# Two-layer graph kernel on one core: random-walk terms applied as R(x·U1 + R·x·U1'), and one stationary operand for q and k

## The chip, the cores and the metric

The kernel runs on one core of one Trainium2 chip. The metric is device time in microseconds; for the kernel before it is the median of three runs, 1678.13 us (1677.03 to 1678.82). One further execution was profiled, and every view of the trace comes from that one. Engines are named as the profile names them: PE is the matrix engine (TensorE), PEld its weight loads, DVE VectorE, ACT ScalarE, POOL GpSimd and SP SyncE, which here only issues transfers.

## The reference, cut to what matters

There are 2708 nodes with 256 features. The first layer mixes two kinds of propagation, a random walk R and a top-p attention A, over two steps; the second layer is a masked graph attention that the change does not touch.

```python
R = S + jnp.eye(N)
R = R / R.sum(-1, keepdims=True)
Z, Xf, Xa = 0, X, X
for n in range(2):
    q = Xa @ W1.T @ W2.T
    k = Xa @ W3.T
    A = top_p(softmax(q @ k.T), 0.9)     # rows cut to 90% of their mass, renormalised
    Xf = R @ Xf
    Xa = A @ Xa
    Z = Z + Xf @ U1[n].T + Xa @ U2[n].T
x = layernorm(X + layernorm(X + Z) * ln_g + ln_b)
# second layer: masked GAT attention over adj, then layernorm
```

So the walk's share of Z is R X U1[0] + R R X U1[1] (with U1 transposed), which is also R (X U1[0] + R (X U1[1])).

## The kernel before, in words

The 2708 rows are cut into 22 tiles, 16 of 128 rows and 6 of 110. Six groups of up to four tiles serve the transposes. The fast path of the first layer is `fast_layer0`; `general_layer0` is a fallback that does not run here.

**Prologue.** x is loaded to `xe`, whose 257th column is one. The loop at line 1039 takes each group: it transposes x (L1045), copies the result to SBUF on ACT and DVE, multiplies it by the stationary `wq` and then by `wk_sb` (L1056) and copies q and k out. `wq` and `wk_sb` each hold their 64 columns twice, so that q and k come out on both halves of the partitions: the scores split the keys in two halves, one on partitions 0 to 63 and one on 64 to 127, and q must stand beside both.

**Attention.** For each tile, `search` is a generator that is advanced one piece per slot: scores (L620) and their exponentials on ACT (L624), in step 1 also a survey on ACT and POOL and a bound on DVE, then candidates and a sort on DVE, and last one pass over the row (L794) that leaves the weights e and their sum. `weigh` then transposes e four tiles at a time (L202), copies the transposes on ACT (L208, `eT`) and multiplies by the features (L217, `att`). It turns group n+1 before it multiplies group n. After each of the six groups it calls `between`, and that calls `slot`. After the last one, ACT scales the result to `xa` (L1005) and the search of the tile three ahead begins.

**Walks.** The generator `walks` (L813) yields one 128-row block product at a time (L845): 2 steps x 22 tiles x 22 blocks = 968 units, each recorded as two matmuls. Its result is in `ps_wk`, a pool of one buffer. Blocks of the adjacency come by SP in half-tiles, one ahead, from a pool of three. In the first walk the moving operand is `xe` with its column of ones, so that the row sums come along; in the second it is `yw`.

**After the first walk** (`after_walk0`, L854): DVE adds the identity's part, `xf`, and takes the reciprocal of the row sum; PE transposes `xf` (L603, shared with the turning of `xa`), ACT copies it, PE multiplies it by both U1 side by side (`terms1`, L890), ACT scales both halves, and POOL adds the own part and x and stores the constant part to DRAM (`c1`). The second half is `yw`. The second walk begins when no such tile is unfinished.

**After the first attention** (`after_attention0`, L869): xa is turned; for every second tile `project` (L586, matmuls L591) makes q and k of the next step with the two stationaries; `terms2` (L905, L910) multiplies by both U2, leaving `ba`, the operand of the second attention, and `c2` in DRAM.

**After the second walk** (`finish`, L919): ACT scales the walk's result straight out of PSUM (L924), POOL sums it with `c1`, `c2` and the held attention result, and two layer norms follow, spread over slots by `yield`; `sources` then prepares the second layer.

**Order of the work.** It is written out by hand: `slot` advances the searches, may begin one, advances the tiles in `doing`, and then issues as many walk units as the slot is given; a walk's end closes the slot and the rest is owed to the next. The four compute engines execute in just this program order. The shares are:

- SPEND_FIRST: 5 units in each of the prologue's slots but the first.
- SPEND_0: 2, 2, 2, 2, 2, 1 for the six slots of a tile in attention step 0.
- SPEND_BETWEEN: 6 in the slots between the steps.
- SPEND_1: 5, 5, 4, 5, 5, 4 for a tile of step 1.

```python
while s and unfinished:
    yield True
...
owed[0] += spend
while owed[0] > 0:
    owed[0] -= 1
    if next(stream, True):
        break
```

Of the kernel before, what the change touches and what calls it, by code (L numbers as in the profile page):

```python
# [36 lines left out]
SPEND_FIRST, SPEND_0 = 5, (2, 2, 2, 2, 2, 1)  # L37
SPEND_BETWEEN, SPEND_1 = 6, (5, 5, 4, 5, 5, 4)
HELD = 8
# [6 lines left out]
def kernel(  # L46
# [71 lines left out]
    def load_x():  # L118
        step = 4
        for t0 in range(0, NT, step):  # L120
            by_tile(xe[:, t0:, 0:D], x, t0, min(t0 + step, NT))
# [103 lines left out]
    def general_layer0():  # L225
        with ExitStack() as l0:
# [8 lines left out]
            load_x()  # L235
# [248 lines left out]
    def fast_layer0(ep, adjp):  # L484
# [22 lines left out]
        wq = w0.tile([P, DC, 2, DA], F32, name="wq")  # L507
        wk_sb = w0.tile([P, DC, 2, DA], F32, name="wk_sb")
# [4 lines left out]
        w2_sb = tmp[:DA, P : 2 * P].rearrange("p (h e) -> p h e", h=2)  # L513
        w1_sb = heldp.tile([P, D], F32, name="xa1")[:DA].rearrange("p (c d) -> p c d", c=DC)
        nc.scalar.dma_start(w1_raw, w1T.rearrange("(c p) e -> p c e", p=P))
        for h in range(2):
            nc.scalar.dma_start(w2_sb[:, h, :], w2T)
        for h in range(2):
            nc.scalar.dma_start(wk_sb[:, :, h, :], w3T.rearrange("(c p) e -> p c e", p=P))
        load_x()  # L520
# [33 lines left out]
        yw = keep.tile([P, NT, D], F32, name="yw")  # L554
# [6 lines left out]
        c2 = [dram.tile([P, D], F32, name=f"c2_{t}") for t in range(NT)]  # L561

# [8 lines left out]
        for c in range(DC):  # L571
            tr = ps_tr.tile([P, 4, P], F32, name="tr")
            nc.tensor.matmul(
                tr[:, 0, :], w1_sb[:, c, :], w2_sb.rearrange("p h e -> p (h e)"),
                start=True, stop=True,
            )
            nc.vector.tensor_copy(wq[:, c].rearrange("p h e -> p (h e)"), tr[:, 0, :])

        def keep_k(s, c0, m, src, copy):
            low = max(0, min(HN - c0, m))  # L580
            if low:
                copy(kT[s][0:DA, c0 : c0 + low], src[0:DA, :low])
            if low < m:
                copy(kT[s][DA:P, c0 + low - HN : c0 + m - HN], src[DA:P, low:m])

        def project(s, c0, w, xT, copy_q, copy_k):  # L586

            pj = ps_tr.tile([P, 4, P], F32, name="tr").rearrange("p (n a) b -> p n (a b)", n=2)
            for n, wm in enumerate((wq, wk_sb)):
                for c in range(DC):  # L590
                    nc.tensor.matmul(  # L591
                        pj[:, n, :w], wm[:, c].rearrange("p h e -> p (h e)"), xT[:, c, :w],
                        start=(c == 0), stop=(c == DC - 1),
                    )
            copy_q(qT[:, c0 : c0 + w], pj[:, 0, :w])
            keep_k(s, c0, w, pj[:, 1], copy_k)
# [216 lines left out]
        def walks():  # L813
# [16 lines left out]
            for n, (s, t, j0, j1) in enumerate(queue):  # L830
                m = rows[t]
                cur, w = (xe, D + 1) if s == 0 else (yw, D)
# [5 lines left out]
                if j0 == 0:  # L838
                    ac = ps_wk.tile([P, CHUNK], F32, name="walk")
                    if s:  # L840
                        ca, cb = (finp.tile([P, D], F32, name=k) for k in ("ca", "cb"))
                        nc.sync.dma_start(ca[:m], c1[t][:m])
                        nc.sync.dma_start(cb[:m], c2[t][:m])
                for j in range(j0, j1):
# [4 lines left out]
                    if j == NT - 1:  # L849
                        doing.append(after_walk0(t, ac) if s == 0 else finish(t, ac, ca, cb))  # L850
# [3 lines left out]
        def after_walk0(t, ac):  # L854
            m = rows[t]
            unfinished.add(t)
            xf = rowp.tile([P, D + 1], F32, name="xf")
            nc.vector.tensor_add(xf[:m], ac[:m, : D + 1], xe[:m, t, :])
            nc.vector.reciprocal(rinv[:m, t : t + 1], xf[:m, D : D + 1])
            yield  # L860
            tp = ps_tr.tile([P, 4, P], F32, name="tr")
            xT = turn(xf, m, tp, nc.scalar.copy)
            yield
            terms1(t, xT)
# [4 lines left out]
        def after_attention0(t, xa):  # L869
# [10 lines left out]
            if t % 2:  # L880
                project(1, off[t - 1], 2 * m, both, nc.scalar.copy, nc.scalar.copy)
                yield
            terms2(t, xT)

        def terms1(t, xT):
# [3 lines left out]
            for c in range(DC):  # L889
                nc.tensor.matmul(  # L890
                    cy[:m], xT[:, c, :m], u_sb[:, 0, c].rearrange("p s e -> p (s e)"),
                    start=(c == 0), stop=(c == DC - 1),
                )
            r = rinv[:m, t : t + 1]
            cs = rowp.tile([P, D], F32, name="cs")
            nc.scalar.activation(cs[:m], cy[:m, 0:D], AF.Copy, scale=r)
            nc.scalar.activation(yw[:m, t, :], cy[:m, D : 2 * D], AF.Copy, scale=r)

            own = rowp.tile([P, D], F32, name="own", bufs=1)
            nc.gpsimd.tensor_scalar(own[:m], yw[:m, t, :], r, None, op0=ALU.mult)  # L900
            nc.gpsimd.tensor_add(cs[:m], cs[:m], own[:m])
            nc.gpsimd.tensor_add(cs[:m], cs[:m], xe[:m, t, 0:D])
# [16 lines left out]
        def finish(t, ac, ca, cb):  # L919
# [4 lines left out]
            nc.scalar.activation(xw, ac[:m, :D], AF.Copy, scale=rinv[:m, t : t + 1])  # L924
            yield
            while t not in held:
                yield
            hh = heldp.tile([P, D], F32, name="hh", bufs=4)[:m]
            nc.gpsimd.tensor_add(ca[:m], ca[:m], cb[:m])
            nc.gpsimd.tensor_add(ca[:m], ca[:m], held.pop(t)[:m])  # L930
            nc.gpsimd.tensor_add(hh, ca[:m], xw)
            yield
            for last in range(2):
# [4 lines left out]
                yield  # L938
# [3 lines left out]
                yield  # L942
# [6 lines left out]
                if not last:  # L949
                    nc.gpsimd.tensor_mul(hh, hh, g_sb[:m])  # L950
                    nc.gpsimd.tensor_add(hh, hh, b_sb[:m])
                    nc.gpsimd.tensor_add(hh, hh, xt)
# [6 lines left out]
        going, doing, unfinished = [], [], set()  # L959
# [33 lines left out]
        def step(s, cur, spend):  # L993
            for t in range(NT):
# [6 lines left out]
                def between(n):  # L1001
                    last = n == len(groups) - 1
                    if last:
                        xa = heldp.tile([P, D], F32, name="xa1")
                        nc.scalar.activation(xa[:m], ac[:m, :D], AF.Copy, scale=rden)  # L1005
                        if s:
# [31 lines left out]

# [273 lines left out]
```

## Time and profile before

| What | Value |
|---|---|
| median of three runs | 1678.13 us |
| the profiled execution: its time, its span | 1677.58 us, 1675.80 us |
| granted PE clock, mean | 0.992 |
| first transposition of attention step 0 starts | 70.46 us |
| last result xa of step 0 | 587.94 us |
| first transposition of step 1 starts | 653.75 us |
| last result xa of step 1 | 1280.04 us |
| one tile of step 0, one of step 1 | 22.3 or 26.1 us in turn; 28.5 us on average |
| walk units issued before step 0, in it, between, in step 1 | 44, 242, 97, 585 |
| POOL transfer c<-cs, issue to landing | 2.1 us |

Times are from the start of the span. The stages are told apart by the starts of the attention's instructions in the trace. A window gives, for each engine, its busy time and the number of its instructions in a stretch; a row of the timeline gives start, length, engine, line, operation and what it writes from what it reads, and in brackets the idle time before it with what ended that. The ends of matmuls are modelled, so a row of matmuls that overlap shows more busy time than they take; the distance from one start to the next does not have that flaw.

### The profile page before, as it was taken

The numbers are of one execution on the slowest core, as the hardware profiler recorded it, in microseconds if no ns is written. First come the engines' busy times: TensorE is split into PE (matmuls) and PEld (weight loads), VectorE is DVE, ScalarE is ACT, GpSimd is POOL, SyncE is SP. The second block draws the span as 40 slices with busy tenths as digits, with TensorE's granted clock in tenths as the row PEclk, the third lists the DMA queues.
The fourth block names the chain that finished last, engine by engine and source line by source line (L and its number), as shares of the span: only waits on it lengthen the run. The fifth ranks groups of instructions, "written<-read, shape, count | busy, mean of one in ns | idle before, by whom it ended". The sixth has DMA issues, their size and how long they took to land.

```text
span 1675.8 us, 23985 instructions
## 1 busy us (share of the span) xinstructions
PE 1610.0 (96%) x8218; PEld 1058.0 (63%) x8218; DVE 1217.0 (73%) x3660; ACT 766.8 (46%) x1324; POOL 423.4 (25%) x893
## 2 busy tenths in 40 slices
PE   7999999999999999999999999999997999999895
PEld 4677777777777776777787878777785222322332
DVE  2954554565455019888999999998994899888886
ACT  1333333333333255656576666667555334243231
POOL 0310111111011023223244444444434020420313
PEclk9999999999999999999999999999999999999998
DMA  6211011111110142212322322323222332232231
GB/s 166 73 47 46 26 43 40 40 31 40 40 43 25 43 104 67 63 49 73 79 72 79 87 68 82 89 58 77 72 65 88 98 99 86 88 93 77 76 86 39
DMA packets 153873, 113.89 MB, mean 68 GB/s; under 512 B 39898, under 2 KB 144094, under 8 KB 153742
## 3 DMA queue, kind: packets, MB, share of 16 engines
q1 hardware_dynamic: 149278, 105.18, 23.4%
q0 software_dynamic: 2112, 5.55, 1.0%
q10 hardware_dynamic: 2352, 1.54, 0.3%
q8 instruction: 67, 1.10, 0.3%
q14 instruction: 64, 0.52, 0.1%
HBM read 101.16 MB, written 11.09 MB: 67 GB/s over the span
## 4 chain that ended last, share of the span: by engine, by line
PE 78%; DVE 9%; ACT 5%; POOL 4%; issue 3%; DMA 0%; ACTq 0%; POOLq 0%; DVEq 0%; SPq 0%
PE att L217 23%; PE walk L845 19%; PE acc L1233 12%; PE acc L1240 6%; PE lg L620 5%; PE tr L202 4%; ACT e L624 3%; PE tr L910 2%; PE tr L890 2%; PE lg L1056 1%; PE tr L591 1%; DVE cand L725 1%; ACT eT L208 1%; DVE scr L791 1%; POOL res L1192 1%
## 5 line engine op out<-in xcount | busy, mean ns | idle before, releaser
L645 ACT ACTIVATE junk<-e,minus,rth 128x2708 bf16<-128x2708 f32 (+1 forms) x88 | 232.8, 2646 | 35.7 <-POOL rth L677 34.6
L845 PE MATMUL walk<-xe,blk 128*128 128x257 f32 (+3 forms) x968 | 240.5, 382 | 0.0
L217 PE MATMUL att<-ba,eT 128*128 128x256 f32 (+3 forms) x968 | 234.1, 383 | 5.0 <-ACT eT L208 5.0
L217 PE MATMUL att<-xe,eT 128*128 128x256 f32 (+3 forms) x968 | 233.3, 381 | 4.3 <-ACT eT L208 4.3
L208 ACT COPY eT<-tr 128x512 f32<-128x512 f32 (+5 forms) x264 | 138.2, 537 | 206.3 <-PE tr L202 206.1
L1233 PE MATMUL acc<-pt,v 128*64 128x512 f32 (+3 forms) x1056 | 226.0, 550 | 4.7 <-DVE pt L1225 3.8
L845 PE MATMUL walk<-yw,blk 128*128 128x256 f32 (+3 forms) x968 | 228.1, 381 | 1.7 <-ACT xw L924 1.7
L725 DVE MAX8 cand<-e 128x8 f32<-128x170 f32 (+1 forms) x352 | 89.2, 322 | 178.8 <-ACT e L624 178.8
L845 PEld LDWEIGHTS walk<-xe,blk 128*128 128x128 f32 (+3 forms) x968 | 174.6, 186 | 54.2 <-issue 29.3
L845 PEld LDWEIGHTS walk<-yw,blk 128*128 128x128 f32 (+3 forms) x968 | 176.7, 186 | 41.5 <-issue 11.5
L1225 DVE SCALAR_TENSOR_TENSOR pt<-e,tj,blk 128x1024 f32<-128x1024 f32 (+3 forms) x176 | 185.8, 1115 | 19.8 <-issue 8.0
L217 PEld LDWEIGHTS att<-ba,eT 128*128 128x128 f32 (+3 forms) x968 | 171.4, 186 | 32.7 <-ACT eT L208 10.0
L217 PEld LDWEIGHTS att<-xe,eT 128*128 128x128 f32 (+3 forms) x968 | 170.9, 186 | 30.9 <-ACT eT L208 7.2
L624 ACT ACTIVATE e<-lg 128x1024 f32<-128x1024 f32 (+1 forms) x132 | 121.1, 921 | 132.3 <-PE lg L620 132.3
L1233 PEld LDWEIGHTS acc<-pt,v 128*64 128x64 f32 (+1 forms) x1056 | 72.1, 137 | 153.5 <-issue 112.3
L202 PE MATMUL tr<-ident,e 128*128 128x128 f32 (+3 forms) x968 | 140.8, 270 | 4.6 <-ACT xT L606 3.8
L202 PEld LDWEIGHTS tr<-ident,e 128*128 128x128 f32 (+3 forms) x968 | 115.1, 139 | 32.3 <-ACT xT L606 6.1
L1165 ACT ACTIVATE blk<-blk 128x1024 f32<-128x1024 f32 (+3 forms) x66 | 63.2, 958 | 155.3 <-DMA blk<-in_adjT_dram 136.3
L1240 PE MATMUL acc<-pt,sb 128*32 128x512 f32 (+3 forms) x1056 | 124.5, 549 | 0.0
L1225 DVE SCALAR_TENSOR_TENSOR pt<-r,tj,blk 128x1024 f32<-128x1024 f32 (+1 forms) x88 | 109.8, 1306 | 10.8 <-issue 7.0
L631 POOL TENSOR_TENSOR fact<-zp 128x1 f32<-128x1 f32 (+1 forms) x44 | 24.8, 563 | 359.0 <-ACT e L624 349.1
L725 DVE MAX8 cand<-scr 128x8 f32<-128x97 f32 (+1 forms) x616 | 101.9, 243 | 0.0
(203 smaller groups left out, 1999.6 us busy)
## 6 DMA issues: line engine op xcount, KB each, us to landing
blk<-in_adjT_dram SPq DMA_DIRECT2D x32, 704.0 KB
blk<-in_adjT_dram SPq DMA_DIRECT2D x32, 512.0 KB
blk<-in_adjT_dram SPq DMA_DIRECT2D x48, 330.0 KB
blk<-in_adjT_dram SPq DMA_DIRECT2D x32, 320.0 KB
blk<-in_adjT_dram SPq DMA_DIRECT2D x12, 605.0 KB
blk<-in_adjT_dram SPq DMA_DIRECT2D x12, 440.0 KB
blk<-in_adjT_dram SPq DMA_DIRECT2D x18, 283.6 KB
c<-cs POOLq DMA_DIRECT2D x32, 128.0 KB, 2.1
```

What stands on the lines that cost most here:

```text
L202: nc.tensor.transpose(tr[: rows[t], q, :m], e[:m, off[t] : off[t + 1]], ident[:m, :m])
L208: copy(eT[:k, : len(grp), :m], tr[:k, : len(grp), :m])
L217: nc.tensor.matmul(acc, eT[: rows[t], q, :m], value(t), start=(t == 0), stop=(t == NT - 1),)
L620: nc.tensor.matmul(lg[:m, h, :w], qT[part, cols], kT[s][part, c0 : c0 + w], start=True, stop=True,)
L624: nc.scalar.activation(halves[:m, :, c0 : c0 + w], lg[:m, :, :w], AF.Exp, accum_out=zp[:m, n : n + 1],)
L645: nc.scalar.activation(junk[:m], e[:m], func, scale=rth, bias=minus1[:m], accum_out=acc)
L725: nc.vector.max(cand[:, n, :], src[:m, n * size : min(N, (n + 1) * size)])
L845: nc.tensor.matmul(ac[:m, :w], blk[: rows[j], j - j0, :m], cur[: rows[j], j, 0:w], start=(j == 0), stop=(j == NT - 1),)
L1165: nc.scalar.activation(bar, bar, AF.Sign)
L1225: nc.vector.scalar_tensor_tensor(pt[:k, :gw], r[h // 2][:k, h % 2, :gw], tj[:k, j, h : h + 1], mask, op0=ALU.max, op1=ALU.mult,)
L1233: nc.tensor.matmul(acc[h // 2][c][q * FO : (q + 1) * FO, :w], v[j][:k, h - 1 + q, :], pts[h - 1 + q][:k, c0 : c0 + w], **at,)
L1240: nc.tensor.matmul(acc[2][c][h * 32 : (h + 1) * 32, :w], sb[:k, j, h : h + 1].to_broadcast([k, 32]), pts[h][:k, c0 : c0 + w], **at,)
```

## The change

The walk is factored. In the prologue, x is loaded to a new tile `xm` instead of `xe`. The transposes of x stay in SBUF as `x_turned`, inside the still unused `ba`, and `terms1` runs for all 22 tiles in the prologue's ten slots, on x itself: its first half, x·U1[0], goes to `c1` in DRAM, and its second, x·U1[1], to `xe`. The first walk therefore carries x·U1[1]; its end, still a DVE add, is scaled by the reciprocal row sum on POOL and added to `c1` into `xm`. The second walk's operand is `xm`. The first attention reads x from `xm`, so the first walk may not end before it is done: no walk unit is issued in the prologue or in step 0, and the shares afterwards are larger.

`finish` now adds the identity's part out of PSUM on DVE and scales on ACT one slot later. It sums x (loaded anew), `c2` and the attention's result. Because the second walk trails the second attention, that result goes to DRAM (`c3`) for the first 18 tiles and is loaded back; the last four are held. Two `yield`s are gone from each of its two layer norms.

For q and k one tile `wkqk` holds W3, the product W1·W2, and W3 again. The stationary is the pair k|q for keys of the first half and q|k for those of the second, so one matmul group gives k on the partitions where it is needed and q on the others; a transfer issued by POOL then copies q to the partitions beside it.

```diff
-SPEND_FIRST, SPEND_0 = 5, (2, 2, 2, 2, 2, 1)
-SPEND_BETWEEN, SPEND_1 = 6, (5, 5, 4, 5, 5, 4)
-HELD = 8
+SPEND_BETWEEN, SPEND_1 = 7, (7, 6, 7, 7, 6, 7)
+HELD, WAITING = 6, 4
...
         nc.scalar.dma_start(w1_raw, w1T.rearrange("(c p) e -> p c e", p=P))
+        nc.scalar.dma_start(w2_sb, w2T)
         for h in range(2):
-            nc.scalar.dma_start(w2_sb[:, h, :], w2T)
-        for h in range(2):
-            nc.scalar.dma_start(wk_sb[:, :, h, :], w3T.rearrange("(c p) e -> p c e", p=P))
-        load_x()
+            nc.scalar.dma_start(wkqk[:, :, 2 * h, :], w3T.rearrange("(c p) e -> p c e", p=P))
+        xm = keep.tile([P, NT, D], F32, name="xm")
+        load_x(xm)
...
+        c3 = {t: dram.tile([P, D], F32, name=f"c3_{t}") for t in range(NT - WAITING)}
...
+        def project(s, c0, w, pj, xT, copy_q, copy_k):
+            for lo, hi, h in ((c0, min(c0 + w, HN), 0), (max(c0, HN), c0 + w, 1)):
+                if lo >= hi:
+                    continue
+                here, there = slice(h * DA, (h + 1) * DA), slice((1 - h) * DA, (2 - h) * DA)
+                at = slice(lo - c0, hi - c0)
                 for c in range(DC):
                     nc.tensor.matmul(
-                        pj[:, n, :w], wm[:, c].rearrange("p h e -> p (h e)"), xT[:, c, :w],
-                        start=(c == 0), stop=(c == DC - 1),
+                        pj[:, at], wkqk[:, c, h : h + 2].rearrange("p h e -> p (h e)"),
+                        xT[:, c, at], start=(c == 0), stop=(c == DC - 1),
                     )
-            copy_q(qT[:, c0 : c0 + w], pj[:, 0, :w])
-            keep_k(s, c0, w, pj[:, 1], copy_k)
+                copy_k(kT[s][here, lo - h * HN : hi - h * HN], pj[here, at])
+                copy_q(qT[there, lo:hi], pj[there, at])
+                nc.gpsimd.dma_start(qT[here, lo:hi], qT[there, lo:hi])
...
-                cur, w = (xe, D + 1) if s == 0 else (yw, D)
+                cur, w = (xe, D + 1) if s == 0 else (xm, D)
...
+                    ca = finp.tile([P, D], F32, name="ca", bufs=4)
                     if s:
-                        ca, cb = (finp.tile([P, D], F32, name=k) for k in ("ca", "cb"))
+                        cb = finp.tile([P, D], F32, name="cb")
+                        nc.sync.dma_start(ca[:m], x[off[t] : off[t + 1], :])
+                        nc.sync.dma_start(cb[:m], c2[t][:m])
+                        if t in c3:
+                            held[t] = finp.tile([P, D], F32, name="cc")
+                            nc.sync.dma_start(held[t][:m], c3[t][:m])
+                    else:
                         nc.sync.dma_start(ca[:m], c1[t][:m])
-                        nc.sync.dma_start(cb[:m], c2[t][:m])
...
             nc.vector.tensor_add(xf[:m], ac[:m, : D + 1], xe[:m, t, :])
-            nc.vector.reciprocal(rinv[:m, t : t + 1], xf[:m, D : D + 1])
+            nc.vector.reciprocal(r, xf[:m, D : D + 1])
             yield
-            tp = ps_tr.tile([P, 4, P], F32, name="tr")
-            xT = turn(xf, m, tp, nc.scalar.copy)
-            yield
-            terms1(t, xT)
+            nc.gpsimd.tensor_scalar(xf[:m, :D], xf[:m, :D], r, None, op0=ALU.mult)
+            nc.gpsimd.tensor_add(xm[:m, t, :], xf[:m, :D], ca[:m])
             unfinished.remove(t)
...
-            nc.scalar.activation(cs[:m], cy[:m, 0:D], AF.Copy, scale=r)
-            nc.scalar.activation(yw[:m, t, :], cy[:m, D : 2 * D], AF.Copy, scale=r)
-
-            own = rowp.tile([P, D], F32, name="own", bufs=1)
-            nc.gpsimd.tensor_scalar(own[:m], yw[:m, t, :], r, None, op0=ALU.mult)
-            nc.gpsimd.tensor_add(cs[:m], cs[:m], own[:m])
-            nc.gpsimd.tensor_add(cs[:m], cs[:m], xe[:m, t, 0:D])
+            nc.scalar.copy(cs[:m], cy[:m, 0:D])
+            nc.scalar.copy(xe[:m, t, 0:D], cy[:m, D : 2 * D])
             nc.gpsimd.dma_start(c1[t][:m], cs[:m])
...
-            nc.scalar.activation(xw, ac[:m, :D], AF.Copy, scale=rinv[:m, t : t + 1])
+            nc.vector.tensor_add(xw, ac[:m, :D], xm[:m, t, :])
             yield
+            nc.scalar.activation(xw, xw, AF.Copy, scale=rinv[:m, t : t + 1])
...
-                        if s:
+                        if s and t in c3:
+                            nc.gpsimd.dma_start(c3[t][:m], xa[:m])
+                            stored.add(t)
+                        elif s:
                             held[t] = xa
...
             for n in range(10):
-                slot(SPEND_FIRST if n else 0, (0, n // 4) if n in (0, 4, 9) else None)
+                slot(0, (0, n // 4) if n in (0, 4, 9) else None)
+                for t in range(n * NT // 10, (n + 1) * NT // 10):
+                    terms1(t, x_turned[:, :, off[t] : off[t + 1]])
             layer1_weights()
-            step(0, xe, SPEND_0)
+            step(0, xm, [0] * len(groups))
```

## The prediction, made before the result was known

> **What bounds the kernel now.** I read the head of the page first, then the busy rows by slice, then windows cut at the stage borders, and last the chain of waits in one stretch of each step. The head:
>
> ```profile
> PE 1610.0 (96%) x8218; PEld 1058.0 (63%) x8218; DVE 1217.0 (73%) x3660; ACT 766.8 (46%) x1324; POOL 423.4 (25%) x893
> ...
> PE   7999999999999999999999999999997999999895
> PEld 4677777777777776777787878777785222322332
> DVE  2954554565455019888999999998994899888886
> ```
>
> TensorE is near full throughout, and VectorE is half idle in attention step 0 (slices 3 to 13) and near full in step 1. The Trainium skill (Perfetto Trace Analysis, "Identifying the Most-Contended Engine") says that matmul busy time is a bad measure of headroom, and to use the weight-load share. By it TensorE has 37% free here, step 1 is VectorE's, and the change pays by spreading walks over VectorE-bound time: step 1 has 562.4 us of DVE work in 626.3. So I tested it with distances between starts, which no modelled end can spoil. Chain of waits, 880 to 900 us (start, length, what):
>
> ```profile
> 883.47 0.86 PE att L217 x4
> 884.34 1.92 PE lg L620 x8
> 886.26 0.37 PE tr L142 x2
> 886.63 1.73 PE walk L845 x8
> 888.36 0.45 PE tr L202 x4
> 888.83 0.59 ACT eT L208
> 889.47 1.99 PE att L217 x8
> ```
>
> A 256-wide fp32 matmul takes 1.73/8 = 0.216 us, a 128-wide transposition 0.11; a 512-wide one 0.43 (L910, 1.72 for four). Counts times these, by stage:
>
> ```profile
> core 0: us, PE busy (x) PEld busy (x) DVE busy (x) ACT busy (x) POOL busy (x), PEclk, DMA share, GB/s
> 0.00:70.46 70.46, 58.76 (x225) 36.18 (x225) 35.18 (x111) 16.73 (x32) 12.00 (x45) 1.00 0.50 130
> 70.46:587.94 517.48, 509.66 (x2443) 376.99 (x2442) 261.70 (x959) 171.94 (x386) 56.70 (x126) 1.00 0.14 39
> 587.94:653.75 65.81, 62.52 (x267) 43.80 (x266) 28.05 (x107) 36.06 (x51) 21.01 (x49) 1.00 0.38 98
> 653.75:1280.04 626.29, 615.24 (x3027) 482.70 (x3026) 562.37 (x2096) 402.25 (x659) 244.52 (x550) 1.00 0.27 70
> ```
>
> Step 0 (second row) holds 968 att (208.6 us), 484 walk (104.6), 484 tr (50.5), 232 score matmuls (43.7: pairs of 64 rows run side by side), 84 L910 (36.0), 44 L890 (18.9), 80 L591 (16.7) and 66 L603 (7.0): 486 of 517.5 us. The between stage comes to 59.4 of 65.8 and step 1 to 589 of 626.3. TensorE's own work fills 94% of layer 0; the row decides against the rule. A moved walk is then worth nothing by itself; a deleted matmul is worth its full length; and stalls (31.5, 6.5, 37 us) are what else can change.
>
> **What is deleted on TensorE.** (a) q and k from one stationary: in the prologue 24 of 48 L1056 matmuls, half of 18.1 us: -9.1. In step 0 and just after, 44 of 88 L591: -9.3. (b) xf is no longer turned: 44 L603 at 0.105: -4.6. (c) One weight transfer less ahead of the first copy; the ACT queue issues it in 0.6 us (two took 1.20): -0.6. The U1 product (88 L890) stays, in another place. Sum -23.6.
>
> **What moves, by stage.**
> Prologue: 70.5 - 0.6 - 9.1; out go 88 walks (-19.0), one L890 set (-1.7), two L603 (-0.2); in come 88 L890-like matmuls (22 tiles x 1.72 = +37.7); fewer seams, -1. It ends at 76.6. ACT has 0.75 us of copies per 1.72 us tile (two of 0.375, as L915/L916), so it hides. The two cs buffers come back after the copy, the issue and the landing (2.1 us for c<-cs): some 2.7 us, against 3.44 us for two tiles of TensorE; hidden, and if not, at most +5.
>
> Step 0: 517.5 - 104.6 (walks) - 18.9 (L890) - 2.3 (22 xf transpositions) - 8.3 (half of L591), and L890's seams, about -2. But the fillers go. The seam between two tiles, before:
>
> ```profile
> 306.37 1.99 PE L620 MATMUL lg<-junk,qT 64*128 64x512 f32 x8
> 307.54 1.03 ACT L624 ACTIVATE e<-lg 128x1024 f32<-128x1024 f32 x1 [0.59 <-PE lg L620]
> 308.56 1.02 ACT L624 ACTIVATE e<-lg 128x1024 f32<-128x1024 f32 x1
> 308.56 0.60 PE L845 MATMUL walk<-xe,blk 128*128 128x257 f32 x2
> 309.00 0.60 PE L202 MATMUL tr<-ident,e 128*128 128x128 f32 x4
> 309.81 0.61 ACT L208 COPY eT<-tr 128x512 f32<-128x512 f32 x1
> 310.47 1.99 PE L217 MATMUL att<-xe,eT 128*128 128x256 f32 x8
> ```
>
> ACT cannot make eT before both exponentials, so att waits until about 3.8 us after the first score matmul, whatever TensorE did meanwhile. Without the two walk matmuls (0.43) it idles 0.43 longer, over some 20 seams: +8.6. Inside a tile the copy (0.59, with 0.2 of latency) has 1.73 + 0.44 us of att and transpositions over it, so no filler is needed. Step 0 becomes 390.
>
> A rule speaks against this: TensorE: Matmul & The Clock Gate (Part 1) says that an idle window of about 3.4 us halves the clock. The PEclk column reads 1.00 with seams of some 0.6 us; the new ones are about 1 us, so I add nothing. By the rule, if gaps did reach it, attention's 16.5 us a tile would double where cold.
>
> Between: 112 half-columns of walk (3 + 13 slots of 7, 224 matmuls) for 97 (194): +6.5; four L890 sets -6.9, xf -0.9, L591 -0.8; the waits for xf vanish (-4.5), but the first search of step 1 took 52 us (601.9 to 653.75) and now has some 47 us of TensorE work over it (13 slots of 3.0 and 7 of scores), so +2 for the part that can't shrink (0 to +5). 61.2.
>
> Step 1: 1712 walks for 1170, +116.8; L890 -10.3, xf -0.9. Seams gain fillers (7, not 4 or 5, a slot): of the 8.1 us that att waits for eT I take 4 off, and 1.2 of L890's. The new wait: ps_wk has one buffer, and now VectorE empties it at all 44 walk ends. Behind that add queue the search steps on DVE, which wait with it; a late add holds the next walk, and in the second walk the scaling on ACT one slot later, with eT copies behind it. Bounds: 0 (adds in the first tiles of step 1 start 0.2 us after the walk, one 3.4) and 44 x 1.2 = 53 (an estimate: the slot with the sort holds six rounds of 0.75 us, L743 and L745, and some 2.5 of small operations, 7 us in all, against 3 us of walks and 2.2 of cover; half of such a lag over all slots). VectorE falls from 90% to about 77% of the step, so I take the nearer row: +2. 729.
>
> Hidden: the q copy by transfer. No row shows one within SBUF; nearest is c<-cs, 2.1 us, 0.65 of POOL. Its reader comes slots later (cover: over 10 us); if scores waited for the last, 0 to +3, and I take 0. POOL queues only tau and survey behind it and behind the c3 issue (waits for xa, 0.65 us for each of 18 tiles): hidden while a search has its two tiles of lead, else 18 x 0.65 = 12. SP's loads come two half-tiles ahead; the walks (44 x 1.39 MB over some 790 us) need 77 GB/s, and 104 went through in one slice. finish loses waits in issue order only; after 1280 us nothing changes: 395.8.
>
> Sum: 76.6 + 390 + 61.2 + 729 + 395.8 = 1652.6 of span, against 1675.8; with the 1.8 us around it (1677.58 - 1675.80) 1654.4. That run lies 0.6 below the median shown. I say 1654.
>
> **Rivals.**
> A, VectorE holds the walk's only PSUM buffer (slower). Place: the 44 walk ends, nearly all in step 1. Price 44 x 1.2 = 53 less the 2 taken: 1705. It outweighs the gain from 0.57 us a walk (25.2/44). For: DVE ran 93% busy from 800 to 1200 us. Against: "DVE e L794" held tr only 0.9 us in all, so VectorE does not trail TensorE by much.
> B, step 0 needs its fillers everywhere: each of 132 slots loses 0.15 us more, +20: 1674. For: the walks (104.6 us) were the only work in step 0 that waited for nothing there. Against: 2.17 us of cover for a copy of 0.8 in each slot.
> C, step 1 was held by VectorE more than starts show (stalls of 37 fall to 20): 1640. For: DVE's row of nines. Against: the 589 us count.
> D, the transfer of q delays each score, 44 x 2.1 less cover: under +3 as placed; inside the main case.
>
> **How the numbers follow.** Main 0.64 (own range 1645 to 1664), C 0.12, B 0.14, A 0.10. Unknown bounds (+5, +3, +12, seams +-9) widen the main case little. 1638 to 1675 leaves A's tail and little else out. A change of 0.2% (3.4 us) is about what measurement tells. Faster: main and C whole, B's half, A's small lags, 0.84; same 0.05; slower 0.11.
>
> **What would show it.** Right: L1056's group gone, one q/k matmul group of 44 in step 0; first tr near 77 us, step 0 ending near 467, step 1 beginning near 528 and ending near 1257; att idle before eT in step 0 doubled to 10 us or so; walk's idle on DVE xf/xw under 5. Wrong: a step-0 tile over 19 us (B), walk waiting on DVE over 20 us in all (A), clock under 0.95 in step 0, or scores released by a qT transfer.

## The result, and the profile after

The kernel after takes 1659.6 us (median of four runs, 1659.51 to 1660.77), the kernel before, on the same chip, 1678.08: a ratio of 0.9892 (95% interval 0.9875 to 0.9909), 18.5 us or 1.1% less. The forecast was 1654, with 1638 to 1675 as its range. The profiled run took 1660.77 us with a span of 1658.8, against 1652.6 in the sum. It is the slowest of the four, 1.2 us above their median, so about 1 us of the stage sums below may belong to this one execution.

The head of the page after and its busy rows:

```profile
PE 1585.9 (96%) x8114; PEld 1043.9 (63%) x8114; DVE 1227.9 (74%) x3682; ACT 754.0 (45%) x1304; POOL 424.0 (26%) x908
...
PE   7999999999999999999999999999998999999894
PEld 3476667666677887787778877887774232222332
DVE  3676667666408877867888888988874989889795
...
PEclk9999999999999999999999999999998999999997
```

TensorE is as full as before, with 104 fewer recorded matmuls. VectorE's row of nines in step 1 has become mostly sevens and eights: its work there is spread over a longer step. Windows cut at the stage borders of the kernel after (start and end, length, then busy time and count for each engine, the granted clock, DMA share and GB/s):

```profile
core 0: us, PE busy (x) PEld busy (x) DVE busy (x) ACT busy (x) POOL busy (x), PEclk, DMA share, GB/s
0.00:77.53 77.53, 66.47 (x199) 30.96 (x200) 39.18 (x123) 29.32 (x72) 18.84 (x67) 1.00 0.51 139
77.53:468.51 390.98, 372.60 (x1855) 269.83 (x1853) 249.78 (x920) 155.71 (x357) 31.85 (x95) 1.00 0.04 11
468.51:530.20 61.69, 59.33 (x263) 45.41 (x263) 28.56 (x110) 32.79 (x40) 15.71 (x43) 1.00 0.43 113
530.20:1255.62 725.42, 719.47 (x3534) 578.76 (x3533) 581.32 (x2140) 395.49 (x633) 274.71 (x582) 1.00 0.35 92
1255.62:1658.80 403.18, 368.08 (x2268) 118.92 (x2266) 329.08 (x390) 140.68 (x205) 82.91 (x121) 0.96 0.30 85
```

| stage | before, us | forecast | after | off by |
|---|---|---|---|---|
| prologue, to the first transposition of e | 70.5 | 76.6 | 77.5 | +0.9 |
| attention step 0 | 517.5 | 390 | 391.0 | +1.0 |
| between the steps | 65.8 | 61.2 | 61.7 | +0.5 |
| attention step 1 | 626.3 | 729 | 725.4 | -3.6 |
| after step 1 | 395.8 | 395.8 | 403.2 | +7.4 |

The first layer came out 1.2 us under its sum. The miss lies in the last row, of which the prediction said that nothing changes. VectorE's share of step 1 fell from 90% to 80% (581.3 of 725.4). Next come the groups that the prediction named. The first line is attention step 0 in the kernel before, the others are the kernel after (line, engine, operation, tiles, count, then busy time and mean ns, then idle time of the engine ahead of them and what ended it):

```profile
L217 PE MATMUL att<-xe,eT 128*128 128x256 f32 (+3 forms) x968 | 233.3, 381 | 4.3 <-ACT eT L208 4.3
...
L216 PE MATMUL att<-xm,eT 128*128 128x256 f32 (+3 forms) x968 | 229.3, 381 | 17.5 <-ACT eT L207 17.5
L216 PE MATMUL att<-ba,eT 128*128 128x256 f32 (+3 forms) x968 | 232.9, 381 | 5.4 <-ACT eT L207 5.4
L852 PE MATMUL walk<-xe,blk 128*128 128x257 f32 (+3 forms) x968 | 223.8, 382 | 1.9 <-DVE xf L866 1.8
L852 PE MATMUL walk<-xm,blk 128*128 128x256 f32 (+3 forms) x968 | 221.8, 380 | 0.0
```

The walks wait 1.9 us for VectorE in all, so the one buffer of `ps_wk` holds nobody up. The idle time ahead of `att` in step 0 is 17.5 us, where it was 4.3. A seam between two tiles of step 0 after, TensorE and ScalarE only:

```profile
274.99 1.99 PE L620 MATMUL lg<-junk,qT 64*128 64x512 f32 x8
276.22 1.03 ACT L624 ACTIVATE e<-lg 128x1024 f32<-128x1024 f32 x1 [0.65 <-PE lg L620]
276.90 1.09 PE L201 MATMUL tr<-ident,e 128*128 128x128 f32 x8
...
277.24 1.02 ACT L624 ACTIVATE e<-lg 128x1024 f32<-128x1024 f32 x1
...
278.23 1.07 ACT L207 COPY eT<-tr 128x512 f32<-128x512 f32 x2
278.87 1.99 PE L216 MATMUL att<-xm,eT 128*128 128x256 f32 x8 [0.88 <-ACT eT L207]
```

As forecast, `att` starts 3.9 us after the first score matmul. Both groups of transpositions are done by then and nothing else is left to issue.

### The profile page after: what moved, and what is told of

It is laid out like the page before. It is cut to its first block, busy times and chain, and to the rows that moved or that the text cites. A ratio compares the mean times of both kernels' runs of the same rounds, so it can differ in the third digit from the quotient of the medians.

```text
span 1658.8 us, 24037 instructions
## 1 busy us (share of the span) xinstructions
PE 1585.9 (96%) x8114; PEld 1043.9 (63%) x8114; DVE 1227.9 (74%) x3682; ACT 754.0 (45%) x1304; POOL 424.0 (26%) x908
## 5 line engine op out<-in xcount | busy, mean ns | idle before, releaser
L216 PE MATMUL att<-xm,eT 128*128 128x256 f32 (+3 forms) x968 | 229.3, 381 | 17.5 <-ACT eT L207 17.5
L1234 PE MATMUL acc<-pt,v 128*64 128x512 f32 (+3 forms) x1056 | 230.7, 555 | 5.1 <-DVE pt L1226 3.8
L852 PE MATMUL walk<-xe,blk 128*128 128x257 f32 (+3 forms) x968 | 223.8, 382 | 1.9 <-DVE xf L866 1.8
L852 PE MATMUL walk<-xm,blk 128*128 128x256 f32 (+3 forms) x968 | 221.8, 380 | 0.0
L216 PEld LDWEIGHTS att<-xm,eT 128*128 128x128 f32 (+3 forms) x968 | 171.2, 186 | 44.8 <-ACT eT L207 22.3
L852 PEld LDWEIGHTS walk<-xm,blk 128*128 128x128 f32 (+3 forms) x968 | 177.7, 186 | 32.7 <-issue 4.9
L201 PEld LDWEIGHTS tr<-ident,e 128*128 128x128 f32 (+3 forms) x968 | 113.7, 139 | 45.1 <-PE lg L620 14.5
L866 DVE TENSOR_TENSOR xf<-walk,xe 128x257 f32<-128x257 f32 (+1 forms) x22 | 9.4, 426 | 112.4 <-PE walk L852 112.4
```

The costliest lines, as they stand in the source:

```text
L201: nc.tensor.transpose(tr[: rows[t], q, :m], e[:m, off[t] : off[t + 1]], ident[:m, :m])
L216: nc.tensor.matmul(acc, eT[: rows[t], q, :m], value(t), start=(t == 0), stop=(t == NT - 1),)
L852: nc.tensor.matmul(ac[:m, :w], blk[: rows[j], j - j0, :m], cur[: rows[j], j, 0:w], start=(j == 0), stop=(j == NT - 1),)
L1234: nc.tensor.matmul(acc[h // 2][c][q * FO : (q + 1) * FO, :w], v[j][:k, h - 1 + q, :], pts[h - 1 + q][:k, c0 : c0 + w], **at,)
```

## The experiments

Eleven kernels were run, each against the kernel before on the same chip. "To acc" is from the end of step 1 to the second layer's first accumulating matmul (`acc`), "rest" from there to the end. The five stage columns are from the profiled run, in us. The kernel before took 1677.1 to 1678.1 us (medians) on the chips used, so a difference of 1 us between two rows says little without the trace.

| run | median | ratio to before (95%) | prologue | step 0 | step 1 | to acc | rest |
|---|---|---|---|---|---|---|---|
| before | 1678.08 | | 70.5 | 517.5 | 626.3 | 18.1 | 377.6 |
| after | 1659.60 | 0.9892 (0.9875-0.9909) | 77.5 | 391.0 | 725.4 | 15.6 | 387.5 |
| apart | 1673.25 | 0.9974 (0.9963-0.9985) | 86.1 | 398.3 | 725.4 | 15.0 | 383.7 |
| stationary | 1660.24 | 0.9898 (0.9882-0.9913) | 61.9 | 510.1 | 626.3 | 18.0 | 377.0 |
| seam | 1638.52 | 0.9764 (0.9751-0.9778) | 77.8 | 369.1 | 725.6 | 15.6 | 387.2 |
| targets | 1665.82 | 0.9932 (0.9918-0.9945) | 77.5 | 391.0 | 725.4 | 24.2 | 382.6 |
| queue | 1658.17 | 0.9881 (0.9866-0.9896) | 77.5 | 391.0 | 725.4 | 15.7 | 385.7 |
| twice | 1668.66 | 0.9940 (0.9927-0.9954) | 84.4 | 390.9 | 725.5 | 15.6 | 388.7 |
| spread | 1658.91 | 0.9889 (0.9874-0.9904) | 78.1 | 391.0 | 725.4 | 15.2 | 385.5 |
| all | 1635.08 | 0.9744 (0.9730-0.9757) | 77.8 | 369.1 | 725.4 | 15.7 | 384.3 |
| warm | 1657.50 | 0.9880 (0.9865-0.9895) | 77.8 | 391.0 | 725.5 | 14.5 | 384.9 |
| pinned | 1663.76 | 0.9916 (0.9903-0.9930) | 77.9 | 390.9 | 725.4 | 25.6 | 381.6 |
| all_warm | 1633.45 | 0.9738 (0.9724-0.9751) | 77.3 | 369.1 | 725.5 | 14.5 | 382.9 |

### Which half of the change carries the gain

**apart** takes the q and k half out of the kernel after:

```diff
-        wkqk = w0.tile([P, DC, 3, DA], F32, name="wkqk")
+        wq = w0.tile([P, DC, 2, DA], F32, name="wq")
+        wk_sb = w0.tile([P, DC, 2, DA], F32, name="wk_sb")
...
-                nc.gpsimd.dma_start(qT[here, lo:hi], qT[there, lo:hi])
```

> The kernel after, with the two stationaries for q and k back (512-wide products for q and for k, no transfer of q); walks stay factored. Theory 1 (deleted TensorE work is worth its full length, a moved walk nothing): +9.1 us before the first score and +9.3 us in step 0 and the stretch behind it, +0.6 us for one more weight transfer, so about 1678 us (1674 to 1682), the time of the kernel before. Theory 2 (the 18 us come from the walks' new place and from the ends of the walks, the q and k products were hidden beside other engines' work): 1660 to 1666 us. In both the stretch after step 1 stays near 403 us.

**stationary** puts only that half into the kernel before, the same lines the other way round.

> The kernel before, with q and k from one stationary and q copied by the transfer; walks as before, nothing moved. Theory 1: 1678.1 - 18.4 - 0.6 = about 1659 us (1656 to 1663), all of the change's gain, and the stretch after step 1 stays near 396 us as in the kernel before; so the walks' factoring comes out at nothing, its deleted transpositions being eaten by empty tile seams and a longer second layer. Theory 2: 1668 to 1677 us.

The second is what theory 1 said, to 1 us: 1660.24, no different from the whole change. Its stages are shorter by 8.5 us (prologue), 7.3 (step 0), 0.7 (between) and 0.7 (after step 1), and step 1 does not move. So one stationary for q and k by itself gives the time of the whole change, and the walks' factoring adds nothing to it. That nothing is two amounts that cancel. Against this run, the kernel after has 15.6 us more in the prologue, 119.2 less in step 0, 3.4 less between and 99.2 more in step 1, which is 7.8 less in the first layer; and it has 8.2 more after step 1. Together +0.4.

The first run fell between the theories: 1673.25 instead of 1678, so the factoring alone does gain, 3.9 us against the kernel before on the same chip. Without the one stationary the first layer loses 16.7 us (8.6, 7.3, 0.7), near theory 1's 19.0, but behind step 1 the run takes 4.5 us less than the kernel after. That pointed to the end of the program, taken up below.

### The seam of step 0

**seam** moves the second product of each tile (`terms2`, 1.7 us of TensorE) from inside the tile into the next tile's seam, between the first two groups of transpositions and the first `att`, with its result in the walk's PSUM buffer, which is free in step 0:

```diff
-            terms2(t, xT)
+            if t < NT - 2:
+                late.append((t, xT))
+            else:
+                terms2(t, xT)
...
                 ahead = turned(n + 1)
+            if seam and n == 0:
+                seam()
```

> The kernel after; in step 0 the second product of each tile (terms2: two 512-wide matmuls with their weights, about 1.7 us of TensorE) is issued between the first two groups of transpositions of the next tile and its first attention matmul, where TensorE waits about 1 us for ScalarE's eT; same work in all. Theory 1 (the seam is empty TensorE time, 20.9 us over 20 tiles beyond the matmuls' own lengths): the stall goes almost whole, 1639 to 1646 us, and step 0 ends about 18 us sooner. Rival (ScalarE or VectorE sets the pace of a step-0 tile, so the wait comes back elsewhere in the tile): 1656 to 1661 us.

The result is 1638.52, 21 us below the kernel after and half a microsecond under the range of theory 1, and step 0 is 21.9 us shorter with the same work in it. One seam of this run:

```profile
245.58 1.99 PE L622 MATMUL lg<-junk,qT 64*128 64x512 f32 x8
247.50 1.09 PE L201 MATMUL tr<-ident,e 128*128 128x128 f32 x8
248.43 1.88 PE L924 MATMUL walk<-u_sb,xT 128*128 128x512 f32 x4
248.85 1.07 ACT L207 COPY eT<-tr 128x512 f32<-128x512 f32 x2
250.14 1.89 PE L218 MATMUL att<-xm,eT 128*128 128x256 f32 x8
```

The product runs under ScalarE's exponentials and copies; `att` follows with no wait. Summed, the wait for eT is gone, and inside the tile, where the product used to lie, none has come in its place:

```profile
L218 PE MATMUL att<-xm,eT 128*128 128x256 f32 (+3 forms) x968 | 227.3, 379 | 0.8 <-ACT eT L207 0.8
```

So a step-0 tile is TensorE's, and needs work in the seam only. That is the term "+0.43, over some 20 seams" of the prediction together with the stall that was there before: counted as the prediction counts, step 0 had 31.5 us of stalls in the kernel before and has about 38.5 in the kernel after. Filling the seam is worth more than the whole change. How much the same filler would gain in the kernel before, no run says.

### After step 1: three causes for 7.4 us

From step 1's end, before against after: the first `acc` comes 2.5 us earlier (15.6 for 18.1); from it to the last of the 264 `pt` operations of VectorE that feed the matmuls it takes 358.1 us for 351.0 (+7.1); from there to the end 29.5 for 26.7 (+2.8). Together +7.4. The 7.1 come in two places: +3.0 by the 22nd `pt` and +4.5 between the 44th and the 66th; what follows gives 0.4 back. With the end of the program that is three places to explain.

**The clock behind the seam.** Windows around the first `acc` (1271.23) in the kernel after (columns as in the stage windows: TensorE's time and count come first, the granted clock is third from the end):

```profile
1263.00:1267.00 4.00, 0.53 (x4) 0.12 (x3) 3.23 (x6) 1.14 (x7) 1.73 (x2) 1.00 0.62 182
1267.00:1271.00 4.00, 2.57 (x6) 1.20 (x6) 4.00 (x4) 1.30 (x8) 0.00 (x0) 0.50 0.23 34
1271.00:1275.00 4.00, 3.77 (x10) 1.25 (x12) 2.96 (x3) 2.28 (x4) 0.00 (x0) 0.50 0.77 250
1275.00:1279.00 4.00, 4.00 (x20) 0.89 (x20) 0.00 (x0) 1.11 (x4) 0.00 (x0) 0.72 0.72 207
```

TensorE is empty for 3.5 us behind step 1, and then the granted clock is 0.50 for 10.2 us (1267.0 to 1277.2). Ten matmuls fit into the four microseconds of the third row. The kernel before had one such stretch between step 1 and its first `acc`, of 3.4 us, behind 3.9 us of empty TensorE:

```profile
1284.00:1288.00 4.00, 0.51 (x5) 0.27 (x3) 2.67 (x5) 1.14 (x7) 3.83 (x6) 1.00 0.73 216
1288.00:1292.00 4.00, 3.38 (x11) 2.42 (x12) 2.67 (x4) 2.13 (x10) 2.59 (x3) 0.57 0.21 68
```

This fits the rule of the Trainium skill (TensorE: Matmul & The Clock Gate, Part 1) that an idle window of about 3.4 us drops the array to half clock; the prediction held it only against step 0, where the rows above agree with it by showing 1.00 for gaps of 0.9 us. The figure is not a safe limit, though. In the second layer TensorE waits 2.5 us for VectorE at one place, in the kernel before as in the kernel after; behind it the clock fell for 3.4 us in the first and stayed at 1.00 in the second:

```profile
1582.00:1586.00 4.00, 4.00 (x8) 0.93 (x7) 2.47 (x7) 0.00 (x0) 2.70 (x4) 0.57 0.10 33
```

```profile
1563.00:1567.00 4.00, 4.00 (x15) 1.22 (x15) 2.48 (x6) 0.00 (x0) 2.59 (x4) 1.00 0.10 33
```

Of the thirteen traces, six show the half clock at that place.

**warm** adds work to test it: 24 transpositions into a buffer that nobody reads, where TensorE waits for the last tile.

```diff
+            if t == NT - 1:
+                busy = ps_tr.tile([P, 4, P], F32, name="tr")
+                for n in range(24):
+                    nc.tensor.transpose(busy[:, n % 4, :], ident, ident)
             yield from sources(t, rowp, ps_tr)
```

> The kernel after, and 24 transpositions of the identity into a buffer that nobody reads, put ahead of the last tile's sources, where TensorE waits 3.5 us behind step 1: work added, none removed, the order of the rest kept. Theory 5 (the 3.5 us of empty TensorE bring 10.2 us of half clock, of which 6 us lie over the second layer's first accumulating matmuls and cost about 3 us): no stretch of half clock between the end of step 1 and the first matmuls, from the first accumulating matmul to the end about 384.5 us instead of 387.5, time 1656 to 1657.5 us. Rival (the clock falls for another reason, or VectorE sets those first neighbours): 1659 to 1662 us.

It gave 1657.5, faster by 2.1 us with more to do. The intervals of the two ratios overlap, but each of its four runs (1657.07 to 1658.73) is below each of the four of the kernel after (1659.51 to 1660.77). The same windows of this run:

```profile
1263.00:1267.00 4.00, 3.42 (x28) 3.01 (x26) 3.23 (x5) 1.14 (x7) 1.73 (x2) 1.00 0.69 195
1267.00:1271.00 4.00, 2.05 (x10) 1.06 (x12) 4.00 (x5) 1.49 (x8) 0.00 (x0) 1.00 0.27 56
1271.00:1275.00 4.00, 4.00 (x28) 1.16 (x28) 3.31 (x3) 1.70 (x2) 0.00 (x0) 1.00 0.84 294
```

The clock stays at 1.00, 28 matmuls fit where there were ten, and the first 22 `pt` take 24.37 us from the first `acc`, as in the kernel before (24.37; 27.35 in the kernel after). The first `acc` comes 1.1 us earlier too, since the last tile's `sources` run at full clock. So the pause is shown to be the cause of the half clock here, and the half clock of the +3.0.

**The second span's targets.** 32 transpositions into `aux` and 16 exponentials on ScalarE were all in the seam behind step 1 before, in seven pieces between the work of the last tiles' `sources`. After, the scheduler, which orders what lies behind the hand-written part, put 8 in the seam and left 24 among the `acc` matmuls of the first span, where the code has them. The last eight before, and the 24 after:

```profile
1295.13 0.60 PE L174 MATMUL aux<-ident,s_src 128*128 128x128 f32 x4
1295.72 1.14 PE L148 MATMUL tr<-wx,xT 128*110 128x264 f32 x4
1296.70 0.60 PE L174 MATMUL aux<-ident,s_src 128*128 128x128 f32 x4
1298.14 1.08 PE L1233 MATMUL acc<-pt,v 128*64 128x512 f32 x4 [0.83 <-issue]
```

```profile
1334.02 1.09 PE L173 MATMUL aux<-ident,s_src 128*128 128x128 f32 x8
1335.04 1.07 PE L1234 MATMUL acc<-pt,v 110*64 110x512 f32 x2
1336.22 1.20 PE L173 MATMUL aux<-ident,s_src 128*128 128x128 f32 x8
1337.35 1.08 PE L1234 MATMUL acc<-pt,v 110*64 110x512 f32 x4
1338.36 1.09 PE L173 MATMUL aux<-ident,s_src 128*128 128x128 f32 x8
```

**targets** holds all of them ahead of the first `acc`, on TensorE and ScalarE, in an order held through the first two neighbours:

```diff
+        r_next = [rp.tile([P, 2, GW], F32, name=f"r{q}") for q in range(2)]
+        pinned = ExitStack()
+        pinned.enter_context(tc.manual_schedule(engines={nc.tensor.engine, nc.scalar.engine}))
+        list(targets(1, r_next, aux))
...
```

> The kernel after; the second layer's targets of its second span (32 transpositions and 16 ScalarE exponentials) are held ahead of the second layer's first accumulating matmul, as the kernel before had them, in the seam where TensorE waits for the second layer's first operands. Theory 1 (their late place, with VectorE waiting 4.9 us for ScalarE's masks, is the larger part of the 7.4 us that the stretch after step 1 is longer than predicted): 1654 to 1657 us, that stretch 398 to 400 us. Rival (the 7.4 us are TensorE's half clock after the seam, or a longer start): 1658 to 1662 us.

This was a miss: 1665.82. From the first `acc` on it is 4.9 us shorter, but the first `acc` comes 8.6 us later: the masks of the second layer stood behind the exponentials on ScalarE, and VectorE waited 13.75 us for one. **pinned** holds TensorE alone, for the first neighbour:

```diff
...
+        pinned.enter_context(tc.manual_schedule(engines={nc.tensor.engine}))
...
```

> The kernel after; on TensorE alone all 32 target transpositions of the second span are held ahead of the first accumulating matmul (8 and 24), ScalarE's order is left free, so that masks come between the exponentials. Theory 4: the 4 us that they cost inside the first span go, and the first accumulating matmul comes 2 to 4 us later since the last of them wait for ScalarE to empty their two buffers: net 0 to -2, 1657.5 to 1660 us. Rival (as in the run with both engines held, the seam pays for all of it): 1663 to 1666 us.

It was slower again, 1663.76, with the first `acc` 9.9 us later and 5.9 us saved behind it; in the seam TensorE waited 6.4 us for ScalarE to empty the buffers. So the seam was not free for them in one block. **spread** gives one tile of targets to each of eight neighbours:

```diff
+                if g == 0 and n == 3:
+                    r_next = [rp.tile([P, 2, GW], F32, name=f"r{q}") for q in range(2)]
+                    later = targets(1, r_next, aux)
+                if g == 0 and n >= 3:
+                    next(later, None)
...
```

> The kernel after; the second layer's targets of its second span (8 tiles, each four transpositions and two ScalarE exponentials) are spread over the fourth to the eleventh neighbour of the first span, one tile each, instead of 8 transpositions in the seam and 24 in one place. Theory 4: clustered, the 16 exponentials hold ScalarE's masks back and VectorE waits 4.9 us; spread, they lie beside 5.5 us of VectorE per neighbour, so from the first accumulating matmul to the end 383 to 385 us instead of 387.5 and the time 1655 to 1657 us. Rival (this stretch is TensorE's, and the transpositions cost the same anywhere): 1659 to 1661 us.

It gave 1658.91, 0.7 us below the kernel after, within the interval. In its trace two of the eight tiles still lie in the seam and six in the span, four transpositions each. The first half clock lasted 6.8 us, not 10.2 (-1.0 by the 22nd `pt`), and the stretch from there to the 66th took 63.5 us for 64.5, where the kernel before takes 60.0. The theory was mostly wrong: VectorE's 4.9 us of waiting was worth 1.0, and 3.5 stay wherever the transpositions lie inside the span. The rival was nearer, and starts show why: each of the six groups puts 1.10 us between two pairs of `acc` matmuls that otherwise start 0.42 apart, 6 x 0.68 = 4.1 us of TensorE. In the kernel before their place in the seam cost nothing behind the first `acc`, and its seam was only 2.5 us longer; no run here brought that order back.

**The closing wait of GpSimd's queue.** Most of what apart had gained lay behind the last instruction that does work. At the program's end GpSimd executes a DRAIN (engine queue, operation, count, shortest/median/longest ns, first and last start). Before, after, and in the run "twice" below:

```profile
L1308 POOLq DRAIN  x3: 40/107/3663, 1671.3 to 1675.5; - x3
```

```profile
L1309 POOLq DRAIN  x3: 40/107/6685, 1651.3 to 1658.5; - x3
```

```profile
L1310 POOLq DRAIN  x3: 40/107/8237, 1657.7 to 1666.5; - x3
```

The longest of each is the closing one. It is 3.66 us after 44 transfers issued by GpSimd, 6.69 after 81 (19 copies of q and 18 stores of c3 more), and everyone waits for it. **queue** issues those 37 from SyncE:

```diff
-                nc.gpsimd.dma_start(qT[here, lo:hi], qT[there, lo:hi])
+                nc.sync.dma_start(qT[here, lo:hi], qT[there, lo:hi])
...
-                            nc.gpsimd.dma_start(c3[t][:m], xa[:m])
+                            nc.sync.dma_start(c3[t][:m], xa[:m])
```

> The kernel after, with the 19 copies of q and the 18 stores of c3 issued from SyncE's queue instead of GpSimd's. Theory 3: the closing wait of GpSimd's queue at the end of the program grows with the number of transfers that GpSimd has issued (3.66 us with 44 before, 5.13 with 62, 5.22 with 63, 6.69 with 81: 0.082 us each), and 3.0 us of the 7.4 us missed after step 1 are that; here the wait is again near 3.66 us, and the time 1656 to 1658 us. Rival (the closing wait is set by something else that changed, or SyncE's queue delays walk loads by as much): 1659 us or more.

The wait was 3.663 us, to the nanosecond that of the kernel before. Of the 3.0 us only 1.4 came off the time (1658.17, just above the theory's range; 1.6 from the last `pt` to the end of the trace), because SyncE, whose own waits for the last stores now ended 2.0 us later, was then the last. **twice** issues each copy of q two times:

```diff
-                nc.gpsimd.dma_start(qT[here, lo:hi], qT[there, lo:hi])
+                for _ in range(2):
+                    nc.gpsimd.dma_start(qT[here, lo:hi], qT[there, lo:hi])
```

> The kernel after, with every copy of q issued twice in a row (19 transfers more, same data). Theory 3: nothing moves before the end of step 1 (the copies land long before the first score that reads them, as the 0.3 us of waiting shows); the closing wait of GpSimd's queue grows by 19 x 0.082 = 1.55 us to about 8.24 us; time about 1661.2 us. Rival (the copy is on the path to the scores): the start of step 0 is 1 to 3 us later and the time 1662 to 1666 us.

The DRAIN was 8.237 us, 1.55 more as forecast. Everything else was a miss: step 0 began 6.8 us later, and the time was 1668.66. From the prologue of this run:

```profile
37.89 3.70 PE L898 MATMUL tr<-u_sb,ba 128*128 128x512 f32 x8
...
44.49 0.37 ACT L903 COPY cs<-tr 128x256 f32<-128x256 f32 x1 [5.67 <-DMA c<-cs]
...
45.19 10.12 PE L898 MATMUL tr<-u_sb,ba 128*128 128x512 f32 x16 [3.60 <-ACT xe L904]
```

The second copy overwrites what the first writes and waits for it, and it waits on GpSimd's queue (19.2 us in the prologue), where the stores of c1 stand behind it. So the `cs` buffers came back late, ScalarE waited 5.67 us for one, TensorE 3.60 us for ScalarE, and the clock was halved for 6.8 us (from 44.4): 16 matmuls took 10.12 us, where eight take 3.70. In the kernel after no wait of this kind appears. The run does not measure the cost of one copy; it shows that this wait in GpSimd's queue in the prologue reached TensorE, and was paid a second time by the clock.

Of the 4.5 us of apart, 1.55 are its 19 transfers less. Another 2.1 lie between the branch at the program's end and GpSimd's next instruction: 0.47 us in apart and in stationary, 2.6 to 2.9 in all the other kernels. The cause of that is open; nothing tried here varied it by itself. The rest, about 1 us, lies ahead of the last `pt`, where apart's half clock was 6.8 us long instead of 10.2. In stationary the branch takes 2.3 us less than in the kernel before, its 19 copies cost 1.55 us more, and the difference is its 0.7 after step 1.

### The edits together

**all** has the edits of seam, queue and spread; **all_warm** those and warm's.

> The kernel after with three edits at once: terms2 in the seam of the next step-0 tile, the transfers of q and c3 on SyncE's queue, the targets spread. If theories 1, 3 and 4 hold their parts add up, since they lie in different stages: 1638.5 - 3 - 4 = about 1632 us (1630 to 1635). If only the seam is real: about 1638.

> The three edits of the run 'all' (terms2 in the step-0 seam, transfers of q and c3 on SyncE's queue, targets spread) and the 24 empty transpositions behind step 1. If theory 5 holds: 1635.1 - 3 = about 1632 us. If not: 1635 to 1636 us.

The first missed its 1632 by 3 us; queue and spread, measured beside it, had fallen short of their forecasts by 1.6 and 3.3 us. The second, at 1633.45, is the fastest here, 2.6% below before; beside all the gain of warm's edit is 1.6 us, within the intervals of the two; in the traces the first 22 `pt` take 24.4 us for 27.0.

## Why the prediction was right, and where it was not

**Which engine.** Right, against the weight-load rule: deleted TensorE work came off the time, 16.6 us of the 19.0 forecast for q and k. Moved work nearly did not: the walks' way through the four stages of the first layer sums to -7.8 us, of which 4.6 are the deleted transpositions of `xf` by the prediction's count; the other 3.2 are the balance of the stalls that changed. The section that the prediction cites names a second measure beside the weight-load share, the achieved share of peak arithmetic (MFU); it was not worked out here.

**Size of (a).** 9.1 + 9.3 + 0.6 were forecast for q and k, the stages of stationary show 8.5 + 7.3 + 0.7, 2.4 us less: 1.2 of it in the prologue, 1.2 in step 0 and behind it. The count was slightly off, as 28 and 48 of these matmuls remain and not 24 and 44: the group that straddles the two halves of the keys is made in two pieces, of the same total width. Which of the deleted products had lain beside a wait no run says.

**The seam term.** The size was right: step 0 came to 391.0 for 390. The sentence that "att idle before eT in step 0" would double to 10 was wrong by its own sum: 4.3 plus 8.6 is 12.9, and it was 17.5. That gap is measured from modelled ends; by starts, the expectation of seam put 20.9 us of stall there, and the run took out 21.9.

**Step 1.** Forecast 729, measured 725.4. The work was right (+106 us by the counts in the trace, where the sum has +116.8 - 10.3 - 0.9), the stalls were not: 37 became about 30, where the sum had 33.8 with the two microseconds for `ps_wk` taken in. Rival A did not happen: 1.9 us of waiting in all. Rival B neither: full tiles of step 0 take 17.6 to 18.9 us, one 19.8 (over the 19 that the prediction took as B's sign), and seam shows that the slots inside need no filler. Rival C happened in small: -3.6 us of the 14 it stood for.

**What luck did.** The first layer's sum is near because its errors have opposite signs: q and k saved 2.4 us less than forecast, the walks 3.6 more. The forecast then lies 5.6 us under the measured median because of the step below.

**The step that failed.** "finish loses waits in issue order only; after 1280 us nothing changes: 395.8." It was 403.2. Three things stood in that sentence's place: a half clock of 10.2 us where there had been 3.4 (+3.0 on the first matmuls), 24 target transpositions moved into the first span by the scheduler (+4.5), and 37 transfers more in GpSimd's closing wait (6.69 us for 3.66, which makes the +2.8 at the end), less 2.5 for an earlier start and 0.4 in the later spans. The transfer of q was costed as hidden: its landing was (scores wait 0.3 us in all for any transfer), and part of its price was paid at the program's end, where the prediction did not look. The clock rule was weighed for step 0 and not for the seam behind step 1, where the profile before already showed a half clock of 3.4 us. No run isolates the earlier start of the first `acc`; 24 transpositions fewer in the seam are one candidate.

## What to carry to other kernels

Where one engine is full, ask of each part of a change whether it deletes that engine's work or moves it, and run the deleting part alone: here it had the time of the whole change. When a change takes fillers out of a stage, look at what its seams become and put other work of the stage there; here that was worth 21 us. Follow the edit to the end of the program: the order of what comes behind, a pause before a dense stretch of matmuls, and the closing wait of a queue can all be set by it.

## What the runs showed of the hardware

GpSimd's closing DRAIN grew by 0.082 us for each transfer that GpSimd had issued: 3.663 us with 44, 5.133 with 62, 5.215 with 63, 6.685 with 81, 8.237 with 100, and all thirteen traces lie on this line. Shortening it pays only until another queue ends last: 3.0 us less of it took 1.4 off the time. And 24 useless transpositions in a 3.5 us pause made the program 2.1 us faster, by keeping the granted clock at 1.00.
